# The order of the second attention's work: fixed slots or a model of the engines

## The chip, the cores and the metric

The kernel runs on one core of a Trainium2 chip. The metric is the device time of one execution in microseconds; what is compared is the median of several executions.

## The reference, cut to what matters

Two layers on x of shape 8 x 512 x 256 (8 batches, 4096 tokens). Each layer normalises x, and adds an attention and a feed-forward part of the same normalised input.

```python
xn = layernorm(x)
x = x + causal_attention_0(xn) + ternary_feed_forward(xn)   # layer 0
xn = layernorm(x)
x = x + attention_1(xn) + expert_choice(xn)                 # layer 1

# attention_1: 16 heads of width 16, 512 tokens a batch
q, k, v = split(xn @ Wqkv.T)
logits = q @ k.T * scale + pos_bias      # pos_bias depends on |i - j| and the head
out = softmax(logits) @ v @ Wout.T       # no mask

# expert_choice: groups of 16 tokens, 64 experts of width 64
sel = gather of the winning token of each group and expert
inter = relu(sel @ f1 + bias) @ f2
out = scatter of inter back to the tokens
```

All of it is computed to full float32 accuracy.

## The kernel before, in words

The program runs in four stages: the first attention (causal), the feed-forward of layer 0, the second attention, and the experts.

An attention is an object of class `Attention`. Its work is cut in 32 **jobs**, one for each batch and each group of four heads. A job has 16 **first products** (`first`, tile `s_ps`, called s below), one for each head r and each tile c of 128 query tokens: queries against all keys in fp32r (one pass), with hi and lo parts of q and k stacked in the rows. VectorE adds the bias and takes the row's least value of the negated logits (the row's maximum, `junk`, then `least`). When all 16 are done, `maxima` splits the minima in two parts (`parts`), transposes them (`m_ps`), copies them (`rows`) and sends them by DMA into two rows of the stacked queries `qs`. Then 16 **second products** (`second`, tile `t_ps`, called t) give logits less their maximum with keys in the partitions. The bias is added from `t_ps` by VectorE (6 of 16) or by a ScalarE copy and a GpSimd addition (10 of 16), both into `pt`; `exp` exponentiates two heads at a time on ScalarE. `weigh` (four concurrent products, `ctx_ps`, called w) multiplies with the values; `take` copies the result (`cx`) and `finish` closes the job: transposes (`tp_ps`), division by the sum (`inv`, `cn`), and for every second and fourth job more transposes (`ct_ps`, `cnT`) and the output product (`o_ps`) which is added to x.

Beside that runs the **preparation** of the next batch: `prep1` normalises, transposes (`xT_ps`), projects to q and k (`proj_ps`), splits into hi and lo parts (`split`) and stores them in DRAM; `values1` makes the values (`v_ps`). `load` fetches the stacks of a job from DRAM, five DMAs on SP's queue.

The banks of PSUM: three for s (`ps_s`), two for t (`ps_t`), one for w (`ps_c`), and two (`ps_m`) that closing and preparation share.

Within attention all engines execute in the order in which the program issues. In the kernel before, `run` issues slots: each slot has one s, one t that is 24 products behind, and where it is due half an exponential pair, a `weigh`, one piece of closing (`close`) and one piece of preparation (`advance`). A generator's `yield` ends a piece; `pause` inserts two empty pieces where a result is waited for.

The experts go in four chunks of two batches. `go_down` makes the second expert product (`d_ps`), copies it out (`down`, three buffers), stores it in DRAM (`inter<-down`, SP's queue), and once a half is there reads it back rearranged (`back<-inter`). `combine` scatters it to the tokens (`y_ps`), adds x and stores the output. This stage's order is left to the build's scheduler.

The token arrays in DRAM between stages (x1d, x2d, x3d, xn1d) are laid out as B*S rows of 256 floats, 1 KB to a row.

Of the kernel before, what the change touches and what calls it, by code (L numbers as in the profile page):

```python
# [62 lines left out]
def block_kernel(ctx: ExitStack, tc: tile.TileContext, a: dict, out: bass.AP):  # L63
# [15 lines left out]

    x = {}  # L80

    def fetch_x(pool, b, src, tag="x", to=x):
        to[b] = pool.tile([P, TPB, D], F32, tag=tag, name="x")
        nc.sync.dma_start(to[b], src[b * S : (b + 1) * S, :].rearrange("(t p) d -> p t d", p=P))

    def leave_x(b, dst):
        nc.sync.dma_start(dst[b * S : (b + 1) * S, :].rearrange("(t p) d -> p t d", p=P), x[b])

    x1d = dram.tile([B * S, D], F32, name="x1d")
    x2d = dram.tile([B * S, D], F32, name="x2d")  # L90
    x3d = dram.tile([B * S, D], F32, name="x3d")
    xnd = dram.tile([B * P, 2 * S], F32, name="xnd")
    xn1d = dram.tile([B * S, D], F32, name="xn1d")
# [17 lines left out]
    nc.gpsimd.memset(power, -0.5)  # L111
# [5 lines left out]
    def norm_steps(layer, b, pool):  # L117
        for t in range(TPB):
            st = pool.tile([P, 6], F32, tag="bn", name="bn")
            nc.vector.bn_stats(st, x[b][:, t, :])  # L120
            nc.vector.bn_aggr(mv[:, layer, b * TPB + t, :], st)
            if t % 2:
                yield
        ve = pool.tile([P, TPB], F32, tag="ve", name="ve")
        nc.vector.tensor_scalar_add(ve, mv[:, layer, b * TPB : (b + 1) * TPB, 1], EPS)  # L125
        yield
        r0 = pool.tile([P, TPB], F32, tag="r0", name="r0")
        nc.gpsimd.tensor_tensor(r0, ve, power, ALU.pow)  # L128
# [3 lines left out]
        nc.vector.tensor_mul(r2, r0, r0)  # L132
        nc.vector.tensor_mul(r2, r2, ve)
        nc.vector.tensor_scalar(r2, r2, -0.5, 1.5, ALU.mult, ALU.add)
        nc.vector.tensor_mul(rstd[:, layer, b * TPB : (b + 1) * TPB], r0, r2)

    def normalise(layer, b, t, dst, src=None):
        i = b * TPB + t
        nc.vector.tensor_scalar(
# [8 lines left out]
    def transpose_steps(srcs, dst, psum, tag, evacuate):  # L148
        for i in range(0, len(srcs), 2):
            ps = psum.tile([P, 2, 2, P], F32, tag=tag, name="xT_ps")  # L150
            for j in range(2):
                for d in range(2):
                    nc.tensor.transpose(ps[:, d, j, :], srcs[i + j][:, d * P : (d + 1) * P], ident)
# [14 lines left out]
    def split(pool, ps, scale, dst, reverse, bufs):  # L168
# [4 lines left out]
        nc.scalar.activation(hi[:, way], ps, AF.Copy, scale=scale)  # L173
# [3 lines left out]
        nc.vector.scalar_tensor_tensor(lo[:, way], ps, scale, hi[:, way].bitcast(F32), ALU.mult, ALU.subtract)  # L177
# [16 lines left out]

    def pause():

        for _ in range(2):
            yield

    class Attention:  # L200
# [4 lines left out]
        def __init__(self, st, causal, order, lag, stacks, qd, kd, bias_of, w_out, fetch, done, cn_bufs):  # L205
# [10 lines left out]
            self.ps_m = pool("ps_m", 2, space=PSUM)  # L216
# [14 lines left out]
            self.jobs = {}  # L231
            if causal:
                self.mask = self.fixed.tile([P, S], F32, name="mask")
                nc.scalar.dma_start(self.mask, a["cst"][:, C_CAUSAL:])
# [7 lines left out]
        def clear(self, i):  # L242

            qs, ks = self.stacks[i]
            nc.gpsimd.memset(qs[64:, :, :].bitcast(F32), 0.0)
            nc.gpsimd.memset(ks[64:, :, :].bitcast(F32), 0.0)
            nc.gpsimd.memset(ks[ROW_M : ROW_M + 2, :, :].bitcast(F32), -1.0)
            if i < len(self.vst):
                nc.gpsimd.memset(self.vst[i], 1.0)


        def keep_v(self, b, t, v_ps, copy=nc.vector.tensor_copy):

            assert b < len(self.vst) or (b - len(self.vst), 3) in self.taken
# [25 lines left out]
        def first(self, s, r):  # L280
# [6 lines left out]
            nc.tensor.matmul(  # L287
# [11 lines left out]
            nc.vector.tensor_tensor_reduce(  # L299
# [3 lines left out]
        def maxima(self, t):  # L303
# [4 lines left out]
            nc.vector.tensor_copy(by_tile[0], job["least"])  # L308
            nc.vector.tensor_tensor(by_tile[1], job["least"], by_tile[0].bitcast(F32), ALU.subtract)
# [4 lines left out]
            nc.tensor.transpose(ps, parts.rearrange("p l r c -> p (l r c)").bitcast(F32), ident)  # L314
            yield True
            rows = self.work.tile([2 * n, P], F32R, tag="rows", name="rows")
            nc.scalar.copy(rows, ps)
            for part in range(2):
                (nc.scalar if self.causal else nc.sync).dma_start(
                    job["qs"][ROW_M + part : ROW_M + part + 1].bitcast(F32), rows[part * n : (part + 1) * n, :].bitcast(F32)  # L320
                )
            yield

        def second(self, n, r):
# [3 lines left out]
            lo = j * P if self.causal else 0  # L328
# [9 lines left out]
            nc.tensor.matmul(  # L338
# [6 lines left out]
            if not self.causal:  # L345
                bias = self.bias_of(self.order[t][1], r, j)
                if r == 0 or (r == 1 and n % 2):
                    nc.vector.tensor_tensor(pt[:, r, :], ps, bias, ALU.add)  # L348
                else:
                    nc.scalar.copy(pt[:, r, :], ps)  # L350
                    nc.gpsimd.tensor_tensor(pt[:, r, :], pt[:, r, :], bias, ALU.add)  # L351
            elif not pair:
                nc.scalar.activation(pt[:, r, lo:], ps[:, lo:], AF.Exp, scale=-1.0)  # L353
            elif r % 2:
                nc.scalar.activation(  # L355
# [5 lines left out]
            if self.causal and r == 3:  # L361

                nc.gpsimd.affine_select(  # L363
# [9 lines left out]
        def exp(self, n, half):  # L373

            pt = self.jobs[n // 4]["p"][n % 4][:, 2 * half : 2 * half + 2, :]
            nc.scalar.activation(pt, pt, AF.Exp, scale=-1.0)  # L376

        def weigh(self, n):
# [5 lines left out]
            for r in range(4):  # L384
                nc.tensor.matmul(  # L385
# [7 lines left out]
        def take(self, t):  # L393

            self.taken.add(self.order[t])
            cx = self.work.tile([P, S], F32, tag="cx", name="cx", bufs=1)
            nc.scalar.copy(cx, self.jobs.pop(t)["ctx"])
            return self.finish(t, cx)

        def finish(self, t, cx):  # L400
# [5 lines left out]
            for c in range(TPB):  # L406
                nc.tensor.transpose(tp[:, c, :], cx[:, c * P : (c + 1) * P], ident)
# [3 lines left out]
            nc.vector.reciprocal(inv, by_head[:, :, :, HD])  # L411
# [3 lines left out]
            nc.vector.tensor_tensor(  # L415
# [14 lines left out]
            for c in range(TPB):  # L430
                nc.tensor.transpose(ps[:, c * P : (c + 1) * P], cn[:, c, :], ident)
            yield True
            nc.scalar.copy(cnT[:, d, :] if self.causal else cnT[:, d, ::-1], ps)
# [781 lines left out]
```

## Time and profile before

| what | value |
| --- | --- |
| three runs | 2197.03, 2205.24, 2216.65 us |
| median | 2205.24 us |
| the profiled execution's own time | 2195.91 us |
| its span, first to last instruction | 2194.2 us |
| mean granted tensor clock | 0.947 |
| busy PE / DVE / ACT / POOL | 88% / 61% / 43% / 28% of the span |
| first attention, about | 0 to 582 us |
| feed-forward | 582 to 1247 us |
| second attention | 1247 to 1937 us |
| experts | 1937 to 2194 us |

The profile is of one execution. Busy shares are over the whole span; the stages differ, so a change in one stage is read from that stage's own stretch of time. Durations of matmuls overlap, since they are pipelined and their ends are modelled: the time from one start to the next is what a matmul takes of the engine. In the lines of the profile, `<-` stands between what is written and what is read, and in brackets is the time for which the engine sat idle before and what ended it.

### The profile page before, as it was taken

To read this page: it belongs to the slowest core of one execution; us is meant where nothing else is said; L and a number is where in the kernel's file an instruction comes from. 1 tells how busy PE (TensorE), PEld (TensorE's weight loads), DVE (VectorE), ACT (ScalarE), POOL (GpSimd) and SP (SyncE) were. 2 spreads that over 40 slices of the span, in tenths; PEclk is the share of its full clock that TensorE was granted. 3 is DMA by queue.
4 is the path that set the end of the run, shared out by engine and by line. 5 is a ranking of instruction groups with operands and counts; after the bars stand their busy time and mean duration, and the time that the engine had idled before them with its cause. 6 is when DMAs were issued, how large, how long until landed. Compare 5 with 4: busy or idle time off the path is not lost.

```text
span 2194.2 us, 29805 instructions
## 1 busy us (share of the span) xinstructions
PE 1930.5 (88%) x10182; PEld 1259.3 (57%) x10182; DVE 1337.9 (61%) x3621; ACT 938.8 (43%) x1570; POOL 610.1 (28%) x552
## 2 busy tenths in 40 slices
PE   3689999999799999999999779999999999968863
PEld 1345555555488888888888544544544444436652
DVE  3667776677345535535535367888878878735431
ACT  0244444445322212212222137777777778834320
POOL 4211111112100000000000256656656657732200
PEclk8799999999899999999999879999999999989986
DMA  5647767674430000000001384554553554167697
GB/s 126 177 121 175 185 164 195 174 173 109 181 127 30 20 10 29 20 1 20 20 1 49 90 238 98 117 124 91 116 127 89 114 121 77 47 235 204 192 254 204
DMA packets 151905, 254.40 MB, mean 116 GB/s; under 512 B 14382, under 2 KB 84911, under 8 KB 151395
## 3 DMA queue, kind: packets, MB, share of 16 engines
q1 hardware_dynamic: 146418, 245.56, 43.2%
q10 hardware_dynamic: 4864, 6.24, 0.9%
q8 instruction: 82, 1.34, 0.3%
q0 software_dynamic: 464, 0.63, 0.1%
q14 instruction: 77, 0.62, 0.1%
HBM read 171.58 MB, written 91.29 MB: 120 GB/s over the span
## 4 chain that ended last, share of the span: by engine, by line
PE 62%; DMA 12%; DVE 10%; ACT 4%; issue 4%; POOL 1%; SPq 1%; ACTq 1%; POOLq 0%; DVEq 0%
PE hid_ps L780 21%; PE t_ps L338 7%; PE ctx_ps L385 7%; PE s_ps L287 6%; PE proj_ps L522 3%; DMA qs<-rows 3%; DVE junk L299 3%; DMA ks<-kd 3%; PE val L780 3%; PE gate L780 3%; PE ffo L780 2%; PE o_ps L443 2%; DMA back<-inter 1%; DMA inter<-down 1%; PE d_ps L1092 1%
## 5 line engine op out<-in xcount | busy, mean ns | idle before, releaser
L287 PE MATMUL s_ps<-ks,qs 96*128 96x512 f32 (+2 forms) x1024 | 471.0, 468 | 81.6 <-DMA ks<-kd 40.4
L351 POOL TENSOR_TENSOR pt<-pt,bias 128x512 f32<-128x512 f32 x320 | 408.8, 1288 | 242.5 <-ACT pt L350 233.5
L338 PE MATMUL t_ps<-qs,ks 128*128 128x512 f32 (+2 forms) x1024 | 394.8, 391 | 38.1 <-DMA qs<-rows 15.1
L299 DVE CUSTOM_DVE_ANT_0 junk<-s_ps,bias 128x512 f32<-128x512 f32 x512 | 338.0, 686 | 120.3 <-PE s_ps L287 107.2
L287 PEld LDWEIGHTS s_ps<-ks,qs 96*128 96x128 f32 x1024 | 201.9, 198 | 265.6 <-DVE least L299 110.7
L299 DVE CUSTOM_DVE_ANT_0 junk<-s_ps,mask 128x384 f32<-128x384 f32 (+3 forms) x512 | 233.1, 486 | 142.0 <-PE s_ps L287 140.8
L338 PEld LDWEIGHTS t_ps<-qs,ks 128*128 128x128 f32 x1024 | 197.9, 195 | 149.1 <-ACT pt L350 43.2
L376 ACT ACTIVATE pt<-pt 128x1024 f32<-128x1024 f32 x256 | 273.7, 1069 | 3.2 <-POOL pt L351 3.1
L770 DVE CAST h<-hf 128x512 fp32r<-128x512 f32 x192 | 81.2, 426 | 303.2 <-ACT hf L819 302.2
L385 PE MATMUL ctx_ps<-pt,vst 128*32 128x512 f32 (+3 forms) x2048 | 262.5, 533 | 3.7 <-ACT pt L376 2.5
L819 ACT ACTIVATE hf<-hid_ps,sh 128x512 f32<-128x512 f32 x128 | 88.1, 688 | 380.5 <-PE hid_ps L780 374.6
L350 ACT COPY pt<-t_ps 128x512 f32<-128x512 f32 x320 | 184.3, 585 | 151.8 <-PE t_ps L338 150.3
L780 PE MATMUL hid_ps<-h,h1T_m 128*128 128x512 f32 x1024 | 237.4, 391 | 0.0
L780 PE MATMUL hid_ps<-h,h2T_m 128*128 128x512 f32 x1024 | 236.9, 392 | 0.0
L780 PEld LDWEIGHTS hid_ps<-h,h2T_m 128*128 128x128 f32 x1024 | 192.2, 188 | 42.6 <-issue 2.9
L780 PEld LDWEIGHTS hid_ps<-h,h1T_m 128*128 128x128 f32 x1024 | 191.2, 188 | 43.8 <-DVE h L771 2.5
L128 POOL TENSOR_TENSOR r<-ve,power 128x4 f32<-128x4 f32 x16 | 16.2, 1012 | 706.9 <-DVE ve L125 602.9
L363 POOL TENSOR_SCALAR_AFFINE_SELECT pt<-pt 128x512 f32<-128x512 f32 x128 | 81.7, 639 | 404.6 <-ACT pt L353 229.6
L353 ACT ACTIVATE pt<-t_ps 128x512 f32<-128x512 f32 (+1 forms) x256 | 130.3, 546 | 99.9 <-PE t_ps L338 95.0
L348 DVE TENSOR_TENSOR pt<-t_ps,bias 128x512 f32<-128x512 f32 x192 | 131.6, 685 | 15.4 <-PE t_ps L338 14.0
L771 DVE TENSOR_TENSOR h<-hf,h 128x512 fp32r<-128x512 f32 x192 | 132.0, 690 | 5.6
L355 ACT ACTIVATE pt<-t_ps 128x256 f32<-128x256 f32 (+1 forms) x128 | 61.9, 491 | 148.3 <-PE t_ps L338 117.1
(137 smaller groups left out, 2265.2 us busy)
## 6 DMA issues: line engine op xcount, KB each, us to landing
qs<-qd SPq DMA_DIRECT2D x128, 256.0 KB
ks<-kd SPq DMA_DIRECT2D x64, 256.0 KB
ks<-kd SPq DMA_DIRECT2D x128, 128.0 KB
inter<-down SPq DMA_DIRECT2D x32, 512.0 KB
back<-inter SPq DMA_DIRECT2D x32, 512.0 KB
qd<-hi SPq DMA_DIRECT2D x32, 256.0 KB
qd<-lo SPq DMA_DIRECT2D x32, 256.0 KB
kd<-hi SPq DMA_DIRECT2D x32, 256.0 KB
```

The costliest lines, as they stand in the source:

```text
L287: nc.tensor.matmul(ps[:, :n], lhsT=job["qs"][:ROW_M, r, c * P : (c + 1) * P], rhs=job["ks"][:ROW_M, r, :n], start=True, stop=True,)
L299: nc.vector.tensor_tensor_reduce(junk[:, :width], ps[:, :width], add, 1.0, 3e38, ALU.add, ALU.min, job["least"][:, c, r : r + 1])
L338: nc.tensor.matmul(ps[:, base - at : S - at], lhsT=job["ks"][:, r, j * P : (j + 1) * P], rhs=job["qs"][:, r, base:], start=True, stop=True,)
L348: nc.vector.tensor_tensor(pt[:, r, :], ps, bias, ALU.add)
L350: nc.scalar.copy(pt[:, r, :], ps)
L351: nc.gpsimd.tensor_tensor(pt[:, r, :], pt[:, r, :], bias, ALU.add)
L353: nc.scalar.activation(pt[:, r, lo:], ps[:, lo:], AF.Exp, scale=-1.0)
L376: nc.scalar.activation(pt, pt, AF.Exp, scale=-1.0)
L385: nc.tensor.matmul(job["ctx"][32 * r : 32 * r + 32, lo:], lhsT=job["v"][:, j, r, :], rhs=job["p"][j][:, r, lo:], start=(j == 0), stop=(j = ...
L771: nc.vector.tensor_tensor(t[1][:, k, :], value, t[0][:, k, :].bitcast(F32), ALU.subtract)
L780: nc.tensor.matmul(ps, lhsT=l, rhs=r, start=(i == 0), stop=(i == len(pairs) - 1))
L819: nc.scalar.activation(hf, ps, AF.Gelu, scale=scales[sc][:, o : o + 1])
```

## The change

Three things change.

First, the second attention is issued by `run_by_clock` instead of `run`. While the program is built, every instruction issued through the wrappers `T_`, `V_`, `A_`, `G_` advances a clock of its engine by an assumed price (`takes`). The loop asks at each step which of s, t, w, closing (c) and preparation (k) could start on PE by these clocks, and issues one by a fixed order of preference. Exponentials are issued when their additions are done by the clocks. s may lead t by up to 40 products. `pause` is empty there. The preparation of a batch starts one batch earlier, when the last job before is begun. `second` keeps the causal case alone, and `second_biased` holds the other.

Second, in the second attention the shared pair of PSUM banks becomes one bank for closing (`ps_m`) and one for preparation (`ps_k`).

Third, x1d, x2d, x3d and xn1d are laid out as in SBUF, 128 partitions by four tokens of 256 floats, so that a partition's four tokens are one run of 4 KB (`tokens`). And in the last chunk of the experts the stores `inter<-down` are issued on ScalarE's DMA queue instead of SP's.

```diff
+    clock = {"PE": 0.0, "DVE": 0.0, "ACT": 0.0, "POOL": 0.0}
+    HANDOVER = 0.6
+    def takes(engine, op, out, k):
+        if engine == "PE":
+            if op == "transpose":
+                return 0.15
+            n = columns_of(k["rhs"]) * (1 if k["rhs"].dtype == F32R else 4)
+            return 0.013 + n / 2400 * (0.25 if k["lhsT"].shape[-1] == 2 * HD else 1)
+        n = columns_of(out)
+        if engine == "DVE":
+            return 0.08 + n / 960
+        if engine == "ACT":
+            return 0.45 if op == "dma_start" else 0.12 + n / 1140
+        return 0.1 if op == "dma_start" else 0.2 + n / (470 if op == "tensor_tensor" else 4700 / 4)
...
+    def tokens(src, b):
+        if src.shape[1] == D:
+            return src[b * S : (b + 1) * S, :].rearrange("(t p) d -> p t d", p=P)
+        return src[b * P : (b + 1) * P, :].rearrange("p (t d) -> p t d", d=D)
-    x1d = dram.tile([B * S, D], F32, name="x1d")
+    x1d = dram.tile([B * P, TPB * D], F32, name="x1d")
...
-            self.ps_m = pool("ps_m", 2, space=PSUM)
+            self.ps_m = pool("ps_m", 2 if causal else 1, space=PSUM)
+            self.ps_k = self.ps_m if causal else pool("ps_k", 1, space=PSUM)
...
+        def run_by_clock(self, extra):
...
+            while w < 4 * jobs or takes or closing or urgent or self.tasks or self.spare:
+                now = clock["PE"]
+                if loaded < jobs and u >= 16 * (loaded - 1) + 5 and v >= 16 * (loaded - 3) and not urgent:
...
+                        self.load(loaded)
+                        self.stack_at[loaded] = now + 8.0
+                        loaded += 1
+                while exps and exps[0][0] <= now + HANDOVER:
+                    self.exp(*exps.popleft()[1:], done_at)
...
+                if u < units and u // 16 < loaded and u - v < 40:
+                    s_at = max(bank_s[u % 3], self.stack_at[u // 16])
+                if v < u and v // 16 in self.rows_at and (v % 4 or v // 4 < w + 3):
+                    t_at = max(self.rows_at[v // 16], self.bank_t[0])
+                if w < 4 * jobs and w in done_at and (w % 4 or not takes):
+                    w_at = done_at[w]
...
+                soon = now + 0.05
+                ahead = clock["DVE"] - now
+                if s_at <= soon and ahead < 0.5:
+                    do = "s"
+                elif w_at <= soon and v // 4 - w >= 2:
+                    do = "w"
+                elif c_at <= soon and urgent:
+                    do = "c"
+                elif k_at <= soon and credit >= 1:
+                    do = "k"
+                elif s_at <= soon and ahead < 1.0:
+                    do = "s"
+                elif t_at <= soon and max(clock["ACT"], clock["POOL"] - 1.0) - now < 1.0:
+                    do = "t"
...
+                else:
+                    nearest = min(s_at, t_at, w_at, c_at, k_at, exps[0][0] if exps else 1e9, takes[0][0] if takes and self.cx_free else 1e9)
+                    clock["PE"] = max(nearest, now + 0.01)
+                    continue
...
-            for step in prep1(b, x_in.pop(b), (xtp, att1.prp), att1.ps_m, "m", wqkv, 2, nc.scalar.copy):
+            for step in prep1(b, x_in.pop(b), (xtp, att1.prp), att1.ps_k, "k", wqkv, 2, A_.copy):
...
-                att1.tasks.append(iter([None] * 10))
                 att1.tasks.append(values1(0))
...
-            if t % 4 == 0 and t // 4 + 1 < B:
-                att1.tasks.append(prep_here(t // 4 + 1))
-            if t % 4 == 2 and t // 4 + 1 < B:
+            if t == 0:
+                att1.tasks.append(prep_here(1))
+            if t % 4 == 3 and t // 4 + 1 < B:
                 att1.tasks.append(values1(t // 4 + 1))
+            if t % 4 == 3 and t // 4 + 2 < B:
+                att1.tasks.append(prep_here(t // 4 + 2))
...
-            att1.run(extra1)
+            att1.run_by_clock(extra1)
...
-                nc.sync.dma_start(half[:, r0 % NH : r0 % NH + NR, :], down)
+                (nc.sync if ch + 1 < B // 2 else nc.scalar).dma_start(half[:, r0 % NH : r0 % NH + NR, :], down)
...
-                    nc.sync.dma_start(xr, x3d[at, :].rearrange("(t p) d -> p t d", p=P))
+                    nc.sync.dma_start(xr, tokens(x3d, b)[:, t : t + 2, :])
```

## The prediction

> **What bounds the kernel now.** I read the windows first, cutting the span where the tensor engine changes its work: first attention to 582 us, feed-forward to 1247, second attention to 1937, mixture of experts to 2194. The built order of the changed kernel is the old one up to the end of the feed-forward; so 690 us of second attention and 257 us of experts are in play. In the windows view the columns are start and end, length, then busy time (and count) of PE, weight loads, DVE, ACT, POOL, then clock, DMA share and GB/s.
>
> ```profile
> 1492.00:1574.00 82.00, 76.09 (x342) 39.92 (x341) 67.75 (x179) 59.56 (x91) 51.28 (x41) 0.96 0.49 110
> 1820.00:1888.00 68.00, 64.17 (x300) 30.84 (x298) 60.33 (x170) 54.87 (x82) 50.38 (x40) 1.00 0.39 79
> 1937.00:2194.00 257.00, 174.97 (x1728) 126.24 (x1728) 98.13 (x156) 67.10 (x132) 42.74 (x40) 0.85 0.83 232
> ```
>
> The first line is one batch of second attention, the second the last batch, which prepares no successor. The chain of waits dates the batches: the same instruction, the second part of a job's minima, returns after five batches.
>
> ```profile
> 1410.53 1.27 DVE parts L309
> ...
> 1819.64 1.27 DVE parts L309
> ```
>
> That is 409.1 us, 81.8 us a batch, with 64 first products (s), 64 second products (t) and 16 weighings (w).
>
> Is PE, busy 76 of 82 us, the bound? In the feed-forward the chain shows 48 one-pass products in a row:
>
> ```profile
> 1228.13 10.94 PE hid_ps L780 x48
> ```
>
> That is 0.228 us each, where the groups give a mean of 0.39: durations overlap. The Trainium skill (Perfetto Trace Analysis, Identifying the Most-Contended Engine) says that matmul occupancy is a poor measure of how full PE is. By the busy row at most 6 us a batch could be won; by spacing much more. I take spacing for every engine:
> - PE: 128 s and t at 0.228 = 29.2; 16 w at 1.0 (one from its start to the next product) = 16; the full-precision work from 14 records of o_ps in 3.30 us in the chain, 0.236 each, two to a product of 256 columns: 8 projection products of 512 columns 7.5; 8 of values 3.8; 8 of output 3.8; eight groups of four transposes at 0.6 = 4.8; minima 0.8. Sum 65.9.
> - DVE: s start 0.61 apart in a row: 64 x 0.61 = 39.0; 24 bias additions 14.6; lo parts 2.4; norms 2.6; closing 2.5; minima 1.4; x 1.2. Sum 63.7.
> - ACT: 40 copies at 0.47 = 18.8; 32 exponentials at 0.95 = 30.4; 14 other copies 6.6; rows 0.8. Sum 56.6.
> - POOL: 40 x 1.29 = 51.6.
>
> So no engine is full: the fullest has work for 65.9 of 81.8 us. The waits of this batch (us, times, longest) say who starves:
>
> ```profile
> DVE junk L299 <- PE s_ps L287: 13.6, 22, 1.2
> ACT pt L350 <- PE t_ps L338: 21.0, 19, 4.2
> ```
>
> and the timeline shows one slot of it:
>
> ```profile
> 1562.87 0.39 PE L338 MATMUL t_ps<-qs,ks 128*128 128x512 f32 x1
> ...
> 1563.07 0.69 DVE L299 CUSTOM_DVE_ANT_0 junk<-s_ps,bias 128x512 f32<-128x512 f32 x1 [0.64 <-PE s_ps L287]
> 1563.10 1.02 PE L890 MATMUL v_ps<-wqkvT,xT 128*128 128x256 f32 x4
> ...
> 1563.78 0.59 PE L287 MATMUL s_ps<-ks,qs 96*128 96x512 f32 x1
> 1564.20 0.40 PE L338 MATMUL t_ps<-qs,ks 128*128 128x512 f32 x1
> ...
> 1564.40 0.69 DVE L299 CUSTOM_DVE_ANT_0 junk<-s_ps,bias 128x512 f32<-128x512 f32 x1 [0.64 <-PE s_ps L287]
> ```
>
> A slot is s, t and one piece of preparation; with that piece it lasts 1.33 us, DVE has one s for it and idles 0.64. Other slots are heavy on DVE and PE waits. One s and one t per slot, whatever else is in it: **second attention is bounded by the sum of slot maxima, not by an engine.**
>
> **The change, part by part.** *Order of second attention.* Nothing is computed more or less: still 512 s and 512 t, and the same closing work. What moves is the order. In the changed build a steady batch reads (P half a projection, V values, X, p, c transposes, o output, m minima) `tstsPtsmPtswoottsoostswtstPstsPptstswtstspPtsPts...`: preparation is parted by two to ten s and t, where before it stood in `PstPst` and `VstVstoostoo`, and s may lead t by 40 products instead of 24. The build's assumed prices are near the spacings: 0.613 against 0.61 for s on DVE, 0.226 against 0.228 for a product, 1.289 against 1.288 for POOL, too dear for ACT copies (0.57 against 0.47), too cheap for w (0.90 against 1.0). It assumes 0.6 us from engine to engine, where the timeline has ACT starting within 0.1 us of a product's end; so real engines run ahead of the plan.
>
> New period: below 65.9 / 0.97 = 68 it can't go, and no better order leaves 81.8. The nearest row is the last batch: without preparation PE has 53.4 and DVE 58.7 us, and it took 68.3, so its fullest engine was used to 86% in strict s-t alternation. Spread preparation and a free choice should use the fullest somewhat better, but two engines are nearly equal here; I take 90%, 73.3, say 73.5: **8.3 us a batch**. First t to last s, 1293 to 1903, is five batches, 1.3 slow ones ahead and the last: 6.3 x 8.3 = 52, and 2 in the last.
>
> *End of attention.* After the last s, 40 t are left instead of 25. In the old tail 25 t take 1903.2 to 1924.0, 0.83 each: +12.5, less 7 for the 15 t missed earlier (0.48 each): +5.5.
>
> *Start.* The first value products now stand behind the first s (`sVssVss`) and need xT, which is queued behind four bias loads; the timeline has DVE waiting for those till 1266.9 already. PE stalls some 4 us there. But job 1's keys arrive only at 1283.4, after 6.5 us of PE idleness, which covers it: between 0 and +5, I take +2.
>
> *Banks.* Preparation gets one bank of its own and closing one, where both shared two. A rule of the skill speaks against this: independent groups should rotate through banks, so that evacuation overlaps the next product (Perfetto Trace Analysis, Matmuls). By the rule, each of the eight turnovers of preparation waits for ACT and DVE, 0.47 + 0.61 and two hand-overs, about 1.3: 10 us a batch, the whole gain. By the row and the order: between two projections stand at least eight s and t with a w and transposes, `ptstswtstsp`, 3.5 us of PE work, longer than 1.3. I take nothing; without that cover it is the fourth case below. In SP's order a minima row still stands behind lo stores and stack loads as before; the rows' wait was 0.4 us a batch, and stays.
>
> *Token arrays* x1d, x2d, x3d, xn1d go from runs of 1 KB to 4 KB (2 KB for x3d's reads). In the experts, DMA is 0.83 busy; a stretch of inter and back reads (1 KB) moves 193 GB/s at share 1.00, one of 4 KB weights 362 at 0.96. 4 MB of xn at 200 against 360 is 21 against 11 us of DMA time, x3d some 5 more; little of it is on the chain (xn 5.6, x3d 4.3 us). Between 0 and -10; I take -3.
>
> *Last chunk's down stores* go from SP's queue to ACT's. The tail:
>
> ```profile
> 2153.40 0.37 SPq L1131 DMA_DIRECT2D out<-x  x1
> 2153.82 1.26 SPq L1108 DMA_DIRECT2D back<-inter  x2
> 2155.18 9.09 SPq L1102 DMA_DIRECT2D inter<-down  x4
> ...
> 2163.17 0.69 DVE L75 COPY down<-d_ps 128x512 f32<-128x512 f32 x1 [9.80 <-DMA inter<-down]
> ```
>
> The second half's stores, whose data was ready from 2147, stand behind back reads and an out store that waits for its addition; the fourth waits for one of three buffers till 2163. On ACT's queue they go at once, and the built order now puts all of go_down ahead of combine(2). The skill (DMA: Bandwidth & Descriptors, Issuing engines are not separate DMA queues) says a second issuing engine saves only issue time. By it, four issues of 0.4: under 2 us. By the row it is not bandwidth but waiting in order: 2147 to 2155, 8 us. DMA is full much of this time, so between -1 and -14; I take -8. ACT has nothing else then.
>
> Sum: -52 - 2 + 5.5 + 2 - 3 - 8 = -57.5, from the profiled execution's 2195.9: 2138. The three runs' median is 2205.2, 9 above it; there I expect **2147 us**.
>
> **Rivals.**
> 1. *Near the engine limit.* s's lead keeps DVE and PE fed to 95%, 69.3 us a batch: 6.3 x 12.5 = 79, with the -5.5 of the other terms -84: 2121. For: priced spacings are right. Against: two engines at 64 and 66 in strict order.
> 2. *The bubbles stay.* Summed over 16 s at a time, the fullest engine's work is much alike in both orders, and DVE still has three banks and t two. At 80 us a batch: -11, in all -17: 2188. Against: those sums are near 68, far from 81.8.
> 3. *Single banks stall PE: slower.* There are 20 turnovers of the two banks a batch (8 of preparation; 4 m, 4 p, 2 c and 2 o of closing). PE stands in order; while it waits for a bank, s and t behind it wait, and DVE drains its three banks in 1.8 us. 0.42 us a turnover eats the 8.3; at 1.0 us the batch takes 93.5, 6.3 x 11.7 = +74, in all +68: 2274. Against: the plan puts a piece off till its evacuation and 0.6 us have passed.
> 4. *The change does nothing*, since the model would reproduce the slots: excluded by the order.
>
> **How the numbers follow.** Forecast 50%, rival 1 20%, rival 2 15%, rival 3 15%. Range: the forecast's period of 71 to 77 with the DMA ends gives 2125 to 2180; rival 1 takes it down to 2090, rival 2 up to 2200, leaving rival 3 and slivers out. 1%, 22 us, is what a measurement of this kernel can tell from no change. Faster: forecast, rival 1 and a quarter of rival 2, 0.74; same 0.12; slower 0.14.
>
> **What would show it.** Right: minima markers 72 to 75 us apart; DVE's wait for s_ps in a batch from 13.6 to below 7; the last down stores issued before 2 us after their copies; a longer t-only tail. Wrong: waits of projections or transposes for `lo`, `hi` or `inv` on PE of over 5 us a batch (rival 3), or 80 us markers with DVE's wait kept (rival 2).

## The result and the profile after

| | before | after |
| --- | --- | --- |
| median of four runs | 2205.2 us | 2231.4 us |
| range | 2197.0 to 2216.7 | 2229.4 to 2241.7 |
| profiled execution, span | 2194.2 us | 2230.6 us |
| second attention, first s to the last store of x3d | 674.2 us | 719.3 us |
| experts, from there to the end | 257.5 us | 254.5 us |
| a batch of second attention (mean of five) | 81.6 us | 85.1 us |
| last s to last t | 23.4 us | 41.3 us |

The changed kernel is **slower**, by 1.5%: ratio 1.0148, 95% interval 1.0108 to 1.0187. Forecast were 2147 us and a ratio below one.

Here and below, an s is dated by the start of the VectorE operation that reads it (`junk`), a t by the first operation that reads its bank. Between the two profiles lie 36.4 us: second attention +45.1, experts -3.0, all that lies ahead of second attention -5.7. The last number says nothing about the kernels: over all profiles below, the last output product of first attention ended anywhere between 573 and 585 us. So only lengths of stages are compared here. The 45.1 divide, by the times of every 64th s, into +3.4 for the first batch, +18.3 for the next six, +4.0 for the last, +17.9 for the tail in which only t is left, and +1.5 after it.

The windows view of the changed kernel, same columns as before (start and end, length, busy time and count of PE, weight loads, DVE, ACT, POOL, then clock, DMA share, GB/s): one batch, the last batch, the experts.

```profile
1576.50:1662.20 85.70, 73.70 (x340) 37.30 (x340) 70.17 (x178) 60.33 (x91) 50.92 (x41) 0.98 0.47 106
1856.30:1923.80 67.50, 57.28 (x273) 27.85 (x273) 60.48 (x158) 52.25 (x79) 46.95 (x38) 0.97 0.32 64
1976.10:2230.60 254.50, 175.84 (x1728) 128.26 (x1728) 96.98 (x156) 67.28 (x132) 43.19 (x40) 0.86 0.83 235
```

PE's busy time fell from 76.1 to 73.7 while the batch grew by 4 us: PE stands idle longer. The last batch, which has no preparation, is as long as before (68.2, now 67.5 between the same minima; the +4.0 above is of the last 64 s, 71.1 us instead of 67.2). The waits of the batch in the first line (us in total, times, longest):

```profile
DVE junk L123 <- PE s_ps L123: 10.2, 11, 2.4
PEld t_ps L123 <- ACT pt L123: 9.2, 18, 1.1
...
DVE pt L123 <- PE t_ps L123: 5.0, 4, 1.7
PE m_ps L123 <- DVE parts L123: 3.9, 3, 1.7
...
PE s_ps L123 <- DMA ks<-kd: 3.5, 2, 3.2
```

(L123 is the wrapper through which all work now passes, so the tiles tell the lines apart.) DVE's wait for s fell from 13.6 to 10.2, but DVE now also waits 5.0 for t. On PE three waits are new or grown: weight loads of t for a bank that ACT empties, minima transposes for `parts`, and s for the keys of the next stack. In the batch of before, the first of them stood at

```profile
PEld t_ps L338 <- ACT pt L350: 4.3, 12, 0.9
```

and the other two were not there. (The preparation of a batch is queued one job, 16 s, earlier than in the slots, not one whole batch.) The chain of the changed kernel shows the second of them:

```profile
1575.40 1.06 DVE parts L123
1576.46 0.02 issue
1576.48 1.21 DVE parts L123
1577.69 0.14 issue
1577.83 0.27 PE m_ps L123
```

After the last s of a job PE goes straight to the transposes and stands until two tiny operations of VectorE are done. The model charges 0.10 us for each of them.

### The profile page after: what moved, and what is told of

It reads as the page before. It is cut to its first block, busy times and chain, and to the rows that moved or that the text cites. A ratio compares the mean times of both kernels' runs of the same rounds, so it can differ in the third digit from the quotient of the medians.

```text
span 2230.6 us, 29823 instructions
## 1 busy us (share of the span) xinstructions
PE 1927.0 (86%) x10182; PEld 1249.8 (56%) x10182; DVE 1356.4 (61%) x3621; ACT 944.5 (42%) x1570; POOL 608.9 (27%) x552
## 5 line engine op out<-in xcount | busy, mean ns | idle before, releaser
L123 PE MATMUL s_ps<-ks,qs 96*128 96x512 f32 (+2 forms) x1024 | 429.3, 433 | 90.1 <-DMA ks<-kd 60.4
L123 POOL TENSOR_TENSOR pt<-pt,bias 128x512 f32<-128x512 f32 x320 | 406.8, 1287 | 288.3 <-ACT pt L123 248.3
L123 PE MATMUL t_ps<-qs,ks 128*128 128x512 f32 (+2 forms) x1024 | 409.7, 416 | 41.9 <-DMA qs<-rows 19.3
L123 DVE CUSTOM_DVE_ANT_0 junk<-s_ps,bias 128x512 f32<-128x512 f32 x512 | 335.3, 684 | 96.5 <-PE s_ps L123 96.3
L123 PEld LDWEIGHTS s_ps<-ks,qs 96*128 96x128 f32 x1024 | 202.2, 199 | 227.3 <-DVE least L123 95.4
L123 DVE CUSTOM_DVE_ANT_0 junk<-s_ps,mask 128x384 f32<-128x384 f32 (+3 forms) x512 | 233.1, 486 | 139.3 <-PE s_ps L123 138.1
L123 PEld LDWEIGHTS t_ps<-qs,ks 128*128 128x128 f32 x1024 | 195.9, 194 | 214.4 <-ACT pt L123 105.6
L123 ACT ACTIVATE pt<-t_ps 128x512 f32<-128x512 f32 (+2 forms) x384 | 192.4, 528 | 246.3 <-PE t_ps L123 215.4
L123 ACT ACTIVATE pt<-pt 128x1024 f32<-128x1024 f32 x256 | 267.6, 1062 | 17.2 <-POOL pt L123 14.7
L123 ACT COPY pt<-t_ps 128x512 f32<-128x512 f32 x320 | 183.0, 584 | 172.6 <-PE t_ps L123 170.2
L123 PE MATMUL ctx_ps<-pt,vst 128*32 128x512 f32 (+3 forms) x2048 | 252.1, 546 | 2.8 <-ACT pt L123 1.9
L123 POOL TENSOR_TENSOR r<-ve,power 128x4 f32<-128x4 f32 x16 | 16.2, 1013 | 703.6 <-DVE ve L123 601.7
L123 POOL TENSOR_SCALAR_AFFINE_SELECT pt<-pt 128x512 f32<-128x512 f32 x128 | 82.0, 640 | 401.5 <-ACT pt L123 401.5
L123 DVE TENSOR_TENSOR pt<-t_ps,bias 128x512 f32<-128x512 f32 x192 | 130.7, 686 | 63.3 <-PE t_ps L123 62.8
L1036 ACT ACTIVATE sg<-gate,s 128x512 f32<-128x512 f32 x64 | 44.2, 690 | 111.5 <-PE gate L1011 107.9
```

The lines of the kernel that those rows point to most:

```text
L123: return f(*args, **k)
L1036: nc.scalar.activation(sg, gate, AF.Silu, scale=scales["s1"][:, o : o + 1])
```

## The experiments

A "batch" below is the mean from s 64 to s 384, the "stage" runs from the first s to the last store of x3d; both are of the profiled run. Ratios are to the kernel before on the same chip.

| kernel | batch | stage | median | ratio, 95% interval |
| --- | --- | --- | --- | --- |
| before | 81.6 | 674.2 | 2205.2 | 1 |
| after | 85.1 | 719.3 | 2231.4 | 1.0148 (1.0108 to 1.0187) |
| e1 side parts only | 81.4 | 672.3 | 2188.0 | 0.9933 (0.9906 to 0.9959) |
| e16 down stores only | 81.8 | 675.6 | 2188.1 | 0.9964 (0.9942 to 0.9986) |
| e2 slots, parted banks | 83.2 | 691.5 | 2212.4 | 1.0046 (1.0029 to 1.0063) |
| e10 after, shared banks | 86.6 | 721.5 | 2234.3 | 1.0162 (1.0127 to 1.0198) |
| e3 after, lead 24 | 84.3 | 694.8 | 2208.6 | 1.0045 (1.0024 to 1.0066) |
| e7 e3, shared banks | 82.5 | 681.7 | 2194.0 | 0.9997 (0.998 to 1.0015) |
| e8 e3, three t banks | 81.0 | 702.4 | 2211.3 | 1.0070 (1.0048 to 1.0091) |
| e4 after, later minima | 85.6 | 731.1 | 2246.0 | 1.0210 (1.0185 to 1.0236) |
| e5 e3, later minima | 84.4 | 709.5 | 2229.9 | 1.0165 (1.0134 to 1.0196) |
| e6 e3, margin 0.2 | 80.4 | 689.1 | 2209.0 | 1.0059 (1.0041 to 1.0077) |
| e13 after, margin 0.2 | 79.5 | 676.6 | 2185.6 | 0.9960 (0.9941 to 0.9979) |
| e17 after, margin 0.4 | 83.0 | 699.5 | 2213.2 | 1.0065 (1.0032 to 1.0098) |
| e18 after, margin 1.0 | 86.2 | 726.4 | 2239.9 | 1.0183 (1.0136 to 1.0230) |
| e9 lead 24, shared, margin 0.2 | 79.4 | 661.3 | 2174.7 | 0.9903 (0.9881 to 0.9925) |
| e14 e9, 20 additions on DVE | 82.5 | 681.9 | 2195.7 | 0.9990 (0.9977 to 1.0003) |
| e15 e9, measured prices | 79.0 | 667.3 | 2183.4 | 0.9934 (0.9917 to 0.9952) |
| e11 light slots | 74.4 | 613.8 | 2132.7 | one run |
| e12 light plan | 72.0 | 597.7 | 2115.0 | one run |

"Margin" is the model's `HANDOVER`; in e9 and e13 to e18 it has the new value from the second batch on.

**The side parts (e1, e16).** The kernel before with `tokens` and the new queue for the last stores, and with the queue alone:

```diff
-nc.sync.dma_start(half[:, r0 % NH : r0 % NH + NR, :], down)
+(nc.sync if ch + 1 < B // 2 else nc.scalar).dma_start(half[:, r0 % NH : r0 % NH + NR, :], down)
```

> The kernel before with the two side parts of the change only: token arrays as in SBUF, and the last chunk's down stores on ScalarE's queue; second attention keeps its slots and its shared banks. My theory: the whole loss is in the order of second attention (its stage grew by 45 us between the traces) and the side parts gain. The feed-forward started 6 us earlier and the experts took 3 us less, so 2205 - 9 = 2196 us. Rival A (the side parts lose, and the stage that grew only inherits it): over 2205, up to 2231. Rival B (the prediction's own terms, -3 and -8): 2194.

> The kernel before with one side part alone: the last chunk's down stores on ScalarE's queue. Together with the token arrays it measured a ratio of 0.9933, 14.7 us. The prediction gave the stores 8 and the arrays 3. If so, the ratio is 0.996. From the changed kernel's trace: its stores were issued 22 us earlier against the end of second attention, but the back reads that follow wait on SP's queue behind an out store, and the final combine began only 4 us earlier: 0.998.

Both gain: 0.9933 together, 0.9964 for the stores alone. That leaves 0.9969 or 7 us for the arrays, but the two intervals overlap, so a gain of the arrays is not shown. (The 0.998 that the trace suggested for the stores is just inside the interval too.) The loss is in the way second attention is issued, and if the parts add, it is larger than the result shows: 1.0148 / 0.9933 is 1.022, some 48 us.

**The banks (e2, e10, e7).**

```diff
-            self.ps_m = pool("ps_m", 2, space=PSUM)
+            self.ps_m = pool("ps_m", 2 if causal else 1, space=PSUM)
+            self.ps_k = self.ps_m if causal else pool("ps_k", 1, space=PSUM)
```

in the slots (e2, preparation takes its banks from `ps_k`), and taken back in the changed kernel at its lead of 40 (e10) and at 24 (e7).

> The kernel before, with the banks of second attention parted as in the changed kernel: one bank for preparation, one for closing, instead of two that both share; order, layouts and queues as before. In the slots a projection follows the one ahead after two slots. My theory (a parted bank costs little, at least where two slots stand between): 2205, within 10 us, PE's waits for hi, lo and xT under 2 us a batch. Rival 3 of the prediction (single banks stall PE): up to 10 us a batch, 2205 + 6.3 x 10 = 2270, with waits of proj_ps for lo or hi of some us a batch.

> The changed kernel as it is (lead 40, 0.6 us), but closing and preparation share their two banks as before the change. Theory (parted banks cost the changed kernel what they cost at lead 24, some 14 us, and what they cost the fixed slots, some 10): 2231 - 14 = 2217, period 85.1 -> 83.3. Rival (at lead 40 other waits hide it): 2231 within 5.

> The changed kernel with the lead capped at 24 and the two banks of second attention shared by closing and preparation again (its order made by the same model). Theory (parting cost 10 us in the fixed slots, through PE standing at proj_ps and o_ps; the model keeps the pieces apart, so here it costs nothing): 2208 within 6 us. Rival (the parted banks cost here too): 2198.

In the slots parted banks cost 0.46%, 10 us, at the edge of what I allowed and a sixth of rival 3. PE's waits in a batch of e2 show two that the batch before lacks, of the output product for x and of a projection for lo:

```profile
PE o_ps L444 <- DVE x L452: 1.4, 1, 1.4
...
PE proj_ps L523 <- DVE lo L177: 0.7, 1, 0.7
```

At lead 24 sharing again gains some 0.5% (the intervals of e3 and e7 don't touch). In the changed kernel as it is, at lead 40, it gains nothing. So parted banks do cost something in two orders of three, but they are not why the changed kernel is slow.

**The lead (e3).** `u - v < 40` becomes `u - v < 24`.

> The changed kernel with the lead of s over t capped at 24 products instead of 40. Theory L (the long lead costs: 40 t alone at the end, and stacks that can't be loaded ahead because four are in use): tail from last s to last t from 41 back to about 25 us, PE's waits of s for ks (4 us a batch) gone: 2231 - 16 - 6 x 4 = 2191 us. Rival P (the period is set by the order around t's two banks and minima, not by the lead): only the tail gains, and what t misses earlier comes back, 2215 to 2231, with periods still at 85 us. Rival B (a shorter lead gives the model less to choose from, bubbles grow): over 2231.

It gained 23 us, 24.5 in the stage, of which the tail is 17.4 (41.3 to 23.9) and a batch only 0.8. The wait for keys is gone, but the minima wait doubled to 6.4 us in this batch of e3:

```profile
PE m_ps L123 <- DVE parts L123: 6.4, 4, 2.4
```

So theory L holds for the tail and the keys, rival P for the period. In the changed kernel s stands at the cap: from s 64 to s 384, the lead was 38 or more at 93% of them. A lead that is always full moves nothing but the start of the tail.

**The minima (e4, e5).**

```diff
 ready_at[kind] = max([clock[e] for e in touched], default=clock["PE"]) + HANDOVER
+if queue is urgent and "DVE" in touched:
+    ready_at[kind] += 2.0
```

> The changed kernel, with the transposes of a job's minima put off by 2 us more on the model's clock after the parts on VectorE. Theory M (the model prices parts at 0.10 us each where the trace has up to 1.2, so PE stands at m_ps, 6 us a batch with its weight load): m_ps waits gone and the period 3 to 6 us shorter, 2231 - 6.3 x 4 = 2206 us. Rival (m_ps only shows where PE would wait anyway, since VectorE is late as a whole): the wait moves to s or t, 2231 within 10.

> The changed kernel with both edits: lead of s over t capped at 24, and a job's minima transposes put off by 2 us more on the model's clock. With the lead at 24 PE still stood 6.1 us a batch at m_ps for the parts. Putting off alone, at lead 40, took that wait away and lost 15 us, with PE's wait for ks grown to 5.8. Theory M2 (the minima wait is real, and was only overtaken by the wait for ks, which the lead of 24 removes): 84.3 - 5 = 79 us a batch, 2208 - 6.3 x 5 = 2177. Rival (what is late is t as a whole: a later minimum makes its job's t later, and VectorE and ScalarE starve in turn): 2208 or more, up to 2223, m_ps wait gone, t's and s's waits grown by as much.

Both theories that made the visible wait the loss fell. The wait for `parts` went, and the time rose by some 14 and 26 us by the ratios, more than even the rivals allowed. In e4 the wait for keys grew (from 4.1 to 5.8 us a batch). In e5, which has no such wait, weight loads of t waited 11.3 us for ACT and DVE 9.1 us for t, where a batch of e3 had 7.2 and 8.3:

```profile
PEld t_ps L123 <- ACT pt L123: 11.3, 18, 1.3
DVE pt L123 <- PE t_ps L123: 9.1, 5, 3.6
```

Later minima mean a later t of that job. The period stayed at 84.4. e5's first batch took 94.6 us against 81.6 in e3, which is 13 of the 14.7 us that its stage lost.

**Three banks for t (e8).** `ps_s` 2, `ps_t` 3, in the pools and in the model.

> The changed kernel with the lead capped at 24, three banks for t and two for s instead of two and three (the model knows it). Theory T (t's two banks pace the order: weight loads of t wait for ACT's or VectorE's release, 8 us a batch, because t's VectorE additions queue behind s on VectorE): period 84.3 -> 80, 2183 us. Rival (VectorE is the scarce one and s needs its three banks): over 2208, PE waits of s for least up by 3 us a batch or more, 2225 to 2250.

The wait changed its place: loads of t for ACT fell from some 8 to 1.4 us a batch (means of five), loads of s for `least` rose from under 1 to some 16, as in this batch:

```profile
PEld s_ps L123 <- DVE least L123: 14.7, 28, 1.0
```

A batch gained 3.3 us, but the first took 102.9, and the time stayed. Neither theory is right as it was put: the banks of t do pace the order, but those taken from s are missed as much.

**The margin (e6, e13, e17, e18).** `HANDOVER` from 0.6 to 0.2 in e6 throughout; in the others only from the second batch on:

```diff
+                    if u == 64:
+                        HANDOVER = 0.2
                     if u % 16 == 0:
                         extra(u // 16)
```

> The changed kernel with the lead capped at 24 and the model's assumed time from engine to engine (HANDOVER) 0.2 instead of 0.6 us; the trace has 0.02 to 0.1. Theory H (the assumed 0.6 makes the model hold t back for its two banks, so that its order is spaced for a slower machine): periods 84.3 -> 80, 2208 - 6.3 x 4 = 2183 us. Rival (in-order engines run ahead of the plan anyway; a smaller margin only makes PE stand at things that are not there yet): 2208 to 2240, with PE waits for parts, lo and pt grown.

> The changed kernel (lead 40, parted banks) with one number altered: the model's time from engine to engine is 0.2 us from the second batch on, 0.6 before. At lead 24 and with shared banks it took a batch from 82.5 to 79.4. Theory H (the 0.6 us is what spaces the changed order): period 85.1 -> 81, 2231 - 5.5 x 4 = 2209 us. Rival (at lead 40 the waits for ks and the minima hold the period): 2225 to 2235.

> The changed kernel with the model's time from engine to engine 0.4 us from the second batch on. With 0.2 a batch took 79.5 us and the whole 2185.6, with 0.6 as changed 85.1 and 2231. Theory H (the margin itself spaces the order): in between, 82 us a batch, 2207 us, ratio 1.005. Rival (each value reshuffles the order, and what comes out is chance): no trend, anywhere from 2180 to 2235.

> The changed kernel with the model's time from engine to engine 1.0 us from the second batch on: the suspected cost nearly doubled. Theory H: 5.6 us a batch for 0.4 us more, as between 0.2 and 0.6, so some 90 us a batch and 2258 us, ratio 1.028. Rival (chance): no trend, 2180 to 2240.

In e6 a batch fell from 84.3 to 80.4, yet the median stayed: its first batch took 105 us, in which t waited 17.6 us for the rows of minima (`qs<-rows`), 14.0 of them at once, where e3 has 5.2. Hence the later start in the others. There **one number takes the changed kernel from 1.0148 to 0.9960**, with the lead, the banks and all prices as they were. The stage is 42.7 us shorter, 35.6 of them in the six batches after the first. A batch of e13, windows and waits:

```profile
1501.50:1581.70 80.20, 73.11 (x340) 38.17 (x340) 67.59 (x178) 60.40 (x90) 50.78 (x40) 0.98 0.46 113
```

```profile
DVE junk L123 <- PE s_ps L123: 8.7, 19, 1.1
...
PEld t_ps L123 <- ACT pt L123: 8.3, 16, 1.1
...
PE s_ps L123 <- DMA ks<-kd: 1.9, 2, 1.5
...
PE m_ps L123 <- DVE parts L123: 0.3, 1, 0.3
```

PE's waits for keys and minima have shrunk from 7.4 to 2.2 us without either being aimed at. Over the doses 0.2, 0.4, 0.6 and 1.0 the batch is 79.5, 83.0, 85.1 and 86.2 us and the ratio rises at every step; from 0.2 to 0.6 the rise is clear of noise, from 0.6 to 1.0 it is not (the intervals overlap). That speaks for a trend and against a lucky order, though it flattens: the last step, 1.1 us a batch, is about a fifth of what I expected.

How the margin does this inside the plan was not taken apart; it enters the release of t's and s's banks, the exponentials, the closing pieces and preparation alike. One thing moves with it: VectorE's two `parts` operations took 2.0, 3.7, 5.2 and 7.0 us a batch at the four doses (the last section has when they are slow). They are not the whole of it, since e7 has 7.5 us of them and a batch of 82.5. Nor is the margin the only way back: lead 24 with shared banks at the full 0.6 (e7) also ends at the time of before, and the two don't add. The smaller margin gains some 41 us at lead 40 and some 21 at lead 24 with shared banks (e7 against e9, next).

**Together, and what holds the rest (e9, e14, e15).** e9 is lead 24, shared banks and the margin of e13. e14 moves four of a batch's additions away from VectorE, e15 alters five prices:

```diff
-if r == 0 or (r == 1 and n % 2):
+if r == 0 or (r == 1 and n % 4 == 1):
```

```diff
 if engine == "DVE":
+    if n <= 4 * TPB and op in ("tensor_copy", "tensor_tensor"):
+        return 0.45
+    if n == D and op == "tensor_scalar":
+        return 0.75
...
-... 0.12 + n / 1140
+... 0.02 + n / 1140
...
-... (0.25 if k["lhsT"].shape[-1] == 2 * HD else 1)
+... (0.31 if k["lhsT"].shape[-1] == 2 * HD else 1)
```

> The changed kernel with what helped so far, together: lead of s over t capped at 24, the two banks shared again, and the model's time from engine to engine 0.2 us, this only from the second batch on (with 0.2 from the start the first batch took 105 us instead of 82, as t stood 14 us for the rows of minima; from the second on a batch took 79 to 80). If these add up: first batch 82, then 78 to 80 us; 2194 - 5.5 x 3 = 2177 us, ratio to before 0.991. Rival (the shared banks and the 0.2 gain on the same wait, VectorE's): no better than the shared banks alone, 2194, ratio 1.000.

> The combined kernel (lead 24, shared banks, 0.2 us from the second batch on), with 20 instead of 24 of a batch's 64 bias additions of t on VectorE and 44 instead of 40 on ScalarE and GpSimd; the model knows it. VectorE gets 4 x 0.61 = 2.4 us less a batch, ScalarE 1.9 and GpSimd 5.2 more. Theory V (with PE's own work near 71 us a batch, VectorE's 67 in order is the second bound): 79.4 -> 78, 2167 us, ratio 0.987. Rival (GpSimd's 57 us or PE now hold it): 2175 or more, ratio 0.990 to 0.995.

> The combined kernel (lead 24, shared banks, 0.2 us from the second batch on), with five prices of the model set to what the traces show: parts 0.45 us each instead of 0.10, a normalisation 0.75 instead of 0.35, w 1.11 instead of 0.90, ScalarE's copies 0.47 instead of 0.57 and exponentials 0.92 instead of 1.02. Theory (the model plans what the chip then doesn't do; with true prices PE's remaining waits for parts, 1.6 us a batch, and for t's banks shrink): 79.4 -> 77, 2161 us. Rival (the order is a greedy choice, its fitting prices matter little): 2175 within 6.

e9 is the fastest kernel here that does the whole work, faster than before and after: 0.9903. But the slots with the side parts alone (e1) have 0.9933, and the intervals of the two overlap: that any planned order beats the slots is not shown. Lead and banks add to the margin in the tail (38.2 to 23.3 us) and not in the period (79.4 against 79.5). e14 lost: theory V fell, and the time rose by more than its rival allowed. By the expectation's estimates ACT and GpSimd took over more than DVE gave up, and DVE's minima parts took 5.3 us a batch instead of 3.6. Measured prices brought nothing (e15's interval reaches from within e9's upward, the period moved by 0.4 us), close to what the rival said.

**PE without its partners (e11, e12).** In the slots of before (e11) and in the order of e7 (e12), `second` ends in

```diff
-if r == 0 or (r == 1 and n % 2):
-    nc.vector.tensor_tensor(pt[:, r, :], ps, bias, ALU.add)
-else:
-    nc.scalar.copy(pt[:, r, :], ps)
-    nc.gpsimd.tensor_tensor(pt[:, r, :], pt[:, r, :], bias, ALU.add)
+nc.scalar.activation(pt[:, r, :], ps, AF.Exp, scale=-1.0)
```

and `exp` does nothing (in e12 the model charges as before).

> The kernel before, order of PE unchanged, with the work between t and the weighing cut down in second attention: no bias is added to t (24 VectorE and 40 GpSimd additions and 40 ScalarE copies a batch left out), and one ScalarE exponential of 512 columns reads each t bank, instead of one of 1024 for a pair. The output is that of another function. In the kernel before, s and t take PE 43.6 us a batch, start to start, where 128 x 0.228 is 29.2. Theory C (the engines that empty the banks set that, VectorE above all): period 81.6 -> 67 to 70. Rival W (PE itself needs 0.34 us for an s or t between different weights): period stays at 78 or more.

> The changed kernel with lead 24 and shared banks, PE's order unchanged (the model still charges for the work left out), with the same work left out as in the light slots: no bias on t, one exponential a t bank. Theory C: period 82.5 -> 67 to 72, the upper end if PE still stands at m_ps for the parts. Rival (the model's order stalls PE by itself, whatever the other engines do): 77 or more.

A batch of e12 in the windows, and two lines of its waits, the largest of PE's weight loads for another engine and the only one of PE itself:

```profile
1629.20:1700.70 71.50, 69.69 (x344) 37.06 (x348) 49.68 (x154) 42.68 (x83) 0.00 (x0) 1.00 0.53 127
```

```profile
PEld t_ps L123 <- ACT pt L446: 8.5, 20, 0.8
...
PE t_ps L123 <- DMA qs<-rows: 1.6, 1, 1.6
```

In the slots the truth lay between theory and rival; in e12 theory C held, at the upper end of its range, but not for the reason given there, since PE itself never stood at `m_ps`. The work left out was worth 10.5 us of e7's batch (82.5 to 72.0) and 7.2 of the slots' (81.6 to 74.4). But with DVE busy 50 and ACT 43 of 71.5 us and GpSimd idle, the batch still took 72.0. With light partners the plan beats the slots by only 2.4 us a batch.

Where PE's time goes, from the start of each of its instructions to the start of the next, charged to the first, us a batch (mean of five; the 43.6 of e11's expectation are 47.2 in this count):

| | s and t | w | all else | batch |
| --- | --- | --- | --- | --- |
| the prediction's sum | 29.2 | 16.0 | 20.7 | 65.9 |
| before | 47.2 | 19.7 | 14.7 | 81.6 |
| after | 52.3 | 17.2 | 15.6 | 85.1 |
| e13, margin 0.2 | 45.1 | 17.7 | 16.7 | 79.5 |
| e12, light plan | 39.1 | 17.0 | 15.9 | 72.0 |

## Why the prediction was wrong, point by point

Two steps failed. The prediction sized PE's floor too low, so the gain that it forecast was not there to be had; and it took the model's hand-over margin for harmless, which made a loss of what gain there was.

- **"PE: 128 s and t at 0.228 = 29.2 ... Sum 65.9."** This term was mis-sized. The 0.228 came from feed-forward products in a row. Here an s or t took 0.305 on the mean in the light plan (39.1 / 128), with PE itself waiting for 1.6 us in the batch shown. The weight loads' waits explain little of it: where neither the next product nor its load waited for another engine (546 of 640), the mean was still 0.297. The next product came 0.23 to 0.24 us later in 306 of the 640 and 0.31 to 0.34 in 172, three quarters of these after a t; what makes the difference is not known. All else was sized 5 us too high, w 1 too low. PE's own work is thus at most 70 to 72 us a batch, so of the 81.6 no 16 us were to be had, but some 10.
- **"I take 90%, 73.3".** With 72 for the fullest engine the same 90% gives 80. e9, e13 and e15 came out at 79.0 to 79.5. The share was fair; what it was taken of was not. None of these orders came near the prediction's 8.3 us a batch; the best saved 2.6.
- **"It assumes 0.6 us from engine to engine ... so real engines run ahead of the plan."** This step took the margin for harmless, and it is enough to decide the sign: setting the number to 0.2 returned 42.7 us of the stage's 45.1.
- **"Bounded by the sum of slot maxima, not by an engine."** Not borne out as the bound: leaving the slots saved 2.4 us a batch at best, with the full work (79.0 in e15 against 81.4 in e1) as with light partners (72.0 against 74.4). So the slots' own cost is a few us a batch; how the rest divides between PE and the engines that empty its banks is shown only as far as the light runs go.
- **End of attention, "+5.5".** It measured +17.9. The 40 t took 41.3 us, more than the assumed rate gives (33.2 at 0.83), and the "less 7 for the 15 t missed earlier" was never returned, as the period grew. Lead 24 took 17.4 back.
- **Start, "+2".** +3.4 in the first batch.
- **Banks, "I take nothing".** In the changed kernel as made, nothing (e10). In the slots 10 us and at lead 24 about as much. So the rule of the Trainium skill (Perfetto Trace Analysis, Matmuls) is seen in two orders, at a price well below the 10 us a batch that the prediction worked out by it: 1.6 and 1.8. Rival 3 as it was put is not what happened: in the changed kernel PE's waits for lo, hi and inv were 0.3 us a batch each at most, those of its weight loads 1.5.
- **Token arrays "-3", down stores "-8".** The stores alone gave 8 us (0.9964, so 3 to 13); the 7 left for the arrays are inside their 0 to -10 but not shown. The mark named for the stores came: in the changed kernel they were issued at once, here from ACT's queue. But the wait moved on. This is the timeline of the changed kernel's tail:

```profile
2180.45 0.59 ACT L77 COPY down<-d_ps 128x512 f32<-128x512 f32 x1 [1.70 <-PE d_ps L1326]
2181.06 0.33 ACTq L1336 DMA_DIRECT2D inter<-down  x1
...
2193.15 0.69 DVE L1364 TENSOR_TENSOR x<-x,y_ps 128x512 f32<-128x512 f32 x1 [4.54 <-DMA x<-x3d]
2193.86 0.37 SPq L1365 DMA_DIRECT2D out<-x  x1
2194.29 8.23 SPq L1342 DMA_DIRECT2D back<-inter  x7
...
2216.53 6.49 PE L1356 MATMUL y_ps<-back,permT 128*32 128x256 f32 x64 [27.58 <-DMA x<-x3d]
```

  Counted from the last x3d store, the last of these stores left at 205 us instead of 227. The back reads, on SP's queue behind an out store that waits for its addition, followed at 218 instead of 230, and the last combine at 240 instead of 244. So 22 us at the stores became 4 at the end, and that the sum met the forecast 8 is partly luck.
- **The rivals.** Rival 2 (bubbles stay, 80 us a batch) was nearest to what the order can do; as planned it was worse than that. Rival 3, the only one on the slow side, was not the right one: it should have read "the planner's assumed hand-over spaces the order for a slower machine".
- **Marks.** Minima 72 to 75 us apart: no, 82 to 88. DVE's wait for s below 7: no, 10.2. Stores: yes. Longer tail: yes.

## What to carry to other kernels

A planner's pessimism is not free: a margin on every hand-over is no slack that fast engines got back here but an order that stays in the program, so measure hand-overs in the trace and try the plan with more and less of it before touching anything else. Take an engine's floor not from the spacing of another stage's products but from a run of the same order with its partners made light, and see what it still waits for there. Compare a new order with the old one that has all the change's other parts, not with the kernel before. And don't remove the wait that the profile shows without asking what paces the batch: here the minima's wait was taken away twice, and the time rose both times.

## What was not expected of the hardware

VectorE's two `parts` operations (128x16) took 0.18 us each wherever no GpSimd bias addition ran beside them (means 180 to 188 ns in six profiles). Beside one they took up to 1.3 us, 0.81 on the mean in the changed kernel (30 of 40) and 0.87 in e14 (28 of 40). The plan decides how many stand beside one: over the doses of the margin 7, 21, 30 and 36 of the 40. The timeline of the changed kernel, with the additions on GpSimd and the two operations:

```profile
1575.13 3.75 POOL L123 TENSOR_TENSOR pt<-pt,bias 128x512 f32<-128x512 f32 x3 [1.83 <-ACT pt L123]
1575.32 1.13 DVE L123 CAST parts<-least 128x16 fp32r<-128x16 f32 x1
1576.48 1.20 DVE L123 TENSOR_TENSOR parts<-least,parts 128x16 fp32r<-128x16 f32 x1
```

and the same operations in the light plan, where GpSimd is idle (ns, least / median / most):

```profile
L123 DVE CAST parts<-least x4: 176/176/177, 1648.2 to 1703.6; 128x16 fp32r<-128x16 f32 x4
L123 DVE TENSOR_TENSOR parts<-least,parts x4: 188/189/192, 1648.4 to 1703.8; 128x16 fp32r<-128x16 f32 x4
```

So work handed to GpSimd can come back as time of VectorE: this fits e14, where moving four additions lost some 20 us, but e14 changed the order as well and does not prove it.
